# Positional convolution of layer 0: shifted copies taken from DRAM, one load for four channel blocks

## The chip, the cores and the metric

The kernel runs on one core of a Trainium2 chip. Time is the device time of one execution in microseconds (us). The kernel before takes 4210.45 us, the median of three runs (4210.17 to 4224.06).

## The reference, cut to what matters

The network has four layers and works on eight images of 256 channels and 32 x 32 pixels. Layer 0 is an attention block with a convolutional feed-forward part behind it. What the change touches is the line `pe`: a depthwise 3x3 convolution of the values `v`, seen as an image, that is added to the attention's output before the projection.

```python
def _attention(x, ...):
    qkv = _bn(_conv1x1(x, qkv_w), ...).reshape(B, NH, 2 * KD + HD, N)
    q, k, v = (qkv[:, :, :KD], qkv[:, :, KD:2 * KD], qkv[:, :, 2 * KD:])
    attn = softmax(einsum('bhkn,bhkm->bhnm', q, k) * SCALE)
    out = einsum('bhdm,bhnm->bhdn', v, attn).reshape(B, Cc, H, W)
    v_img = v.reshape(B, Cc, H, W)
    pe = _bn(_dwconv3(v_img, pe_w), ...)      # 3x3, one filter per channel
    out = out + pe
    return _bn(_conv1x1(out, proj_w), ...)
```

With B = 8 images, NH = 4 heads, KD = 32 and 64 value channels per head, an image has 256 value channels and N = 1024 pixels. Every output channel of `pe` depends on nine pixels of one input channel.

## The kernel before, in words

Layer 0 is the function `fast0`. Channels lie on the 128 partitions, two tiles of them (c = 0, 1), pixels in the free dimension, and everything is float32. A TensorE instruction of float32 leaves two records in the profile, so the counts of records in it are twice those in the code.

**The loops.** `attention` goes through 128 steps: 8 images, two halves gq of the 512 query columns, eight blocks kt of 128 keys. A step has four score matrix products `s` (L1393; 32 rows x 128 columns of the array each, one per head), two exponentials `e` on ScalarE (L1399), eight products `A` (L1357; 128 rows x 32 columns each, four column groups for the heads, two channel tiles) for the step before, and two sums on VectorE (L1353). `finish` divides by the sums, adds the result to `o`, projects, and stores to `mids`.

`before_attention(b)` prepares an image: it loads it, normalizes it (L1217 squares it into the space of `v`), projects it to `v`, `q`, `k` (L1276 to L1287), transposes `v` (L1297), and then makes the positional convolution into `o`, in four groups (c, h): a channel tile and a half of the pixels. A group works like this. A tile `thrice` of 96 partitions holds three copies of 32 channels, shifted by minus one, zero and plus one image row, for four channel blocks g side by side in the free dimension. GpSimd zeroes the row beyond the image's edge (L1307), SyncE issues twelve loads from `v` in SBUF (L1312; one per shift j and block g, 32 partitions x 512 or 480 pixels), and twelve matrix products `pe` (L1324; 96 rows x 32 columns, three horizontal shifts times four blocks, each block in its own column group) add up all nine taps. ScalarE takes the result out (L1327). There is one buffer for `thrice`, so the copies for a group wait for the products of the group before.

`before_gates`, `gates` and `transforms` are the feed-forward part: a projection `pi`, depthwise filters on VectorE (L1246), a gate, a transfer through DRAM (`gated`), a projection `po` (L1491), and small matrix products for the Fourier filter (`fwd`, `back`).

**The order of the work.** These generators are put side by side by `by_time`: each has a start and a step, and the one that is due next gives the next piece of code. Below that, the framework's scheduler sets the order of instructions on each engine when the program is built, from its own estimate of when each operand is there. Each engine then runs its queue in that fixed order and stops at an instruction whose semaphores are not there. All plain loads and stores of this part go through SyncE's one queue, in order.

In the order as built, the first group of each image and, from image 2 on, the first three groups have their twelve `pe` products together. In the groups 2 to 4 of images 0 and 1 and in the fourth group of the other images, some of them are mixed, one to four at a time, with products `A`, `s` or `po`.

Of the kernel before, what the change touches and what calls it, by code (L numbers as in the profile page):

```python
# [10 lines left out]
F32 = mybir.dt.float32  # L11
# [6 lines left out]
P = 128  # L18
B = 8
C = 256  # L20
KC = C // P
N = 1024
HF = 512
# [113 lines left out]
def img(ap):  # L137
    return ap.rearrange("p (h w) -> p h w", w=IMG)
# [971 lines left out]
def fast0(net, io):  # L1110
    tc, nc = net.tc, net.nc
# [6 lines left out]
    with ExitStack() as ctx, ExitStack() as att:  # L1118
# [6 lines left out]
        awp = io.pool(att, "f0aw", 1)  # L1125
        aone = io.pool(att, "f0aa", 1)
# [7 lines left out]
        g, bb, m, v = (vec[:, i * nb : (i + 1) * nb] for i in range(4))  # L1134
# [13 lines left out]
        s, t = st[:, :nb], st[:, nb:]  # L1148

        wpe = net.load(awp, "f0_wpe").rearrange("p (k t g o) -> p k t g o", k=KC, t=3, g=4)  # L1150
        pib = wp.tile([P, 8], F32, name="pib")
        gain = net.load(wp, "l0_gam2")

        def bank(name):
            return own["X"].tile([P, HF], F32, tag="X", name=name)

        with ExitStack() as tmp:
# [13 lines left out]
            for j in range(8):  # L1171
                for k in range(KC):
                    nc.tensor.matmul(
                        ps[:, 4 + j : 5 + j], lhsT=wpi[:, k, bass.ts(j, P)], rhs=n2b(k),
                        start=(k == 0), stop=(k == KC - 1),
# [25 lines left out]

        qs, ks, vas, os = ({} for _ in range(4))

        mids = [net.dpool.tile([P, KC, N], F32, tag=f"mid{b}", name=f"mid{b}") for b in range(B)]
        gated = [net.dpool.tile([P, 4, 4, 2, P], F32, tag=f"gated{b}", name=f"gated{b}") for b in range(B)]

        def sc(i):
            return s[:, i : i + 1]

        def sh(i):  # L1210
            return t[:, i : i + 1]

        def normed(xn, x, sq):

            squares = [sq(k) for k in range(KC)]
            for k in range(KC):
                nc.scalar.activation(squares[k], x[:, k, :], AF.Square)  # L1217
            yield
            ps = bank("ms")
            for k in range(KC):  # L1220
                for h in range(2):
                    nc.tensor.matmul(
                        ps[64 * h : 64 * h + 64], lhsT=net.mean64, rhs=squares[k][:, bass.ts(h, HF)],
                        start=(k == 0), stop=(k == KC - 1),
                    )
            r = one.tile([P, HF], F32, tag="r", name="r")
            net.rsqrt(r, ps, net.eps6)
            yield
            for h in range(2):
                pr = bank("rb")  # L1230
                nc.tensor.matmul(
                    pr, lhsT=net.unit[64 * h : 64 * h + 1, :], rhs=r[64 * h : 64 * h + 1, :], start=True, stop=True
                )
                nc.scalar.copy(squares[0][:, bass.ts(h, HF)], pr)
            nc.vector.tensor_tensor(xn, x, squares[0].unsqueeze(1).to_broadcast([P, KC, N]), ALU.mult)
# [33 lines left out]
        def before_attention(b):  # L1269
            xn = aone.tile([P, KC, N], F32, tag="xn", name="xn")  # L1270
            nc.sync.dma_start(out=xn, in_=io.src[b])
            yield
            v = aone.tile([P, KC, N], F32, tag="v", name="v")
            yield from normed(xn, xn, lambda k: v[:, k, :])
            yield
            def projected(d, w, j, norm):  # L1276
                for h in range(2):
                    ps = bank("qkv")
                    net.linear(ps, w, xn, bass.ts(j, P), bass.ts(h, HF))
                    nc.scalar.activation(d[:, bass.ts(h, HF)], ps, AF.Identity, scale=sc(norm), bias=sh(norm))  # L1280

            for c in range(KC):
                projected(v[:, c, :], wv, c, 2 + c)
                yield
            for d, (j, name) in ((qs, (0, "q")), (ks, (1, "k"))):
                d[b] = atwo.tile([P, N], F32, tag=name, name=name)
                projected(d[b], wqk, j, j)  # L1287
                yield

            va = vas[b] = atwo.tile([P, NT, KC, P], F32, tag="va", name="va")  # L1290
            for t4 in range(0, NT, 4):
                for t2 in (t4, t4 + 2):
                    ps = bank("vT")
                    for i in range(2):
                        for c in range(KC):
                            lo = i * C + c * P
                            nc.tensor.transpose(ps[:, lo : lo + P], v[:, c, bass.ts(t2 + i, P)], net.ident)  # L1297
                    nc.scalar.copy(va[:, t2 : t2 + 2].rearrange("p t c d -> p (t c d)"), ps)
                yield

            o = os[b] = atwo.tile([P, KC, N], F32, tag="o", name="o")
            for c in range(KC):
                for h in range(2):

                    thrice = aone.tile([96, 4, HF], F32, tag="thrice", name="thrice")
                    edge = thrice[0:32, :, :IMG] if h == 0 else thrice[64:96, :, HF - IMG :]
                    nc.gpsimd.memset(edge, 0.0)  # L1307
                    for j in range(3):
                        n = HF * h + IMG * (j - 1)
                        lo, hi = max(0, n), min(N, n + HF)  # L1310
                        for g in range(4):
                            nc.sync.dma_start(  # L1312
                                out=thrice[32 * j : 32 * j + 32, g, lo - n : hi - n],
                                in_=v[32 * g : 32 * g + 32, c, lo:hi],
                            )
                    yield
                    ps = bank("pe")
                    for j, s_ in enumerate((0, -1, 1)):
                        for g in range(4):
                            to, fr = (  # L1320
                                img(a)[:, :, max(0, -d_) : IMG - max(0, d_)]
                                for a, d_ in ((ps[32 * g : 32 * g + 32], s_), (thrice[:, g, :], -s_))
                            )
                            nc.tensor.matmul(  # L1324
                                to, lhsT=wpe[:96, c, s_ + 1, g, :], rhs=fr, start=(j == 0), stop=(j == 2)
                            )
                    nc.scalar.activation(  # L1327
                        o[:, c, bass.ts(h, HF)], ps, AF.Identity, scale=sc(4 + c), bias=sh(4 + c)
                    )
                    yield  # L1330
                yield
# [189 lines left out]
        for b in range(B):  # L1521
            streams += [
                (T * (b - 1) - 2, 32 / 21, before_attention(b)) if b > 1 else (11 * b, 1.0, before_attention(b)),
                (T * (b + 1) + 7.4, 0.9, before_gates(b)),
                (T * (b + 1) + 10.5, 32 / 44, gates(b)),
                (T * (b + 2) + 11.5, 2, transforms(b)),
            ]
# [1438 lines left out]

GENERAL = [layer0, layer1, layer2_attention, layer2_ffn, layer3_attention, layer3_experts]
LAYERS = [fast0, fast1, fast2, fast2f, fast3, fast3e]
LEAST, MOST = 1e-25, 1e25

# [114 lines left out]
def pack(i):  # L3085

    d = {"x": i["x"].reshape(B, C, N)}
# [40 lines left out]
    p = np.arange(P)  # L3128
# [49 lines left out]
    cols += [_cols(z[n]) for n in ("norm1_w", "norm1_b", "norm2_w", "norm2_b", "gamma1")]  # L3178

    taps = z["pe_w"][v_of].reshape(KC, 4, 32, 3, 3)  # L3180
    wpe = np.zeros((3, 32, KC, 3, 4, 32), np.float32)
    for ch in range(32):
        wpe[:, ch, :, :, :, ch] = taps[:, :, ch].transpose(2, 0, 3, 1)
    d["f0_wpe"] = wpe.reshape(96, -1)
    cols.append(z["dw_w"].reshape(8, P, 9).transpose(1, 0, 2).reshape(P, -1))
    d["f0_vec"] = np.concatenate(cols, 1)

# [48 lines left out]
```

## Time and profile before

| | |
|---|---|
| median of 3 runs | 4210.45 us |
| the profiled execution | 4221.38 us, span 4219.6 us |
| granted TensorE clock, mean | 0.952 |
| layer 0's attention in the span | from about 50 us to beyond 1100 us |
| `pe` products | 768 records, 130.7 us busy |
| period of an image in the middle of the layer | 158 to 160 us |

In the lines of the profile, PE is TensorE's matrix products and PEld its weight loads, DVE VectorE, ACT ScalarE, POOL GpSimd, SPq the queue of SyncE. A line of the timeline gives start and duration in us, the engine, the line of code, the operation with its output and inputs, the shape, and after x how many of them were merged in the line; in brackets stands how long the engine was idle before, and for whom it waited. For a matrix product `96*32` gives the rows and columns of the array that it takes.

### The profile page before, as it was taken

Reading aid. Unit: us, or ns where it says so; the run is one execution under the profiler, and the core shown is the slowest. Engines: PE = TensorE matmul, PEld = TensorE weight load, DVE = VectorE, ACT = ScalarE, POOL = GpSimd, SP = SyncE. Lnnn points to the kernel's source line nnn. Section 1 sums busy time; section 2 is a strip of 40 time slices with the busy share of each in tenths; the row PEclk is TensorE's granted clock in tenths of the full one; section 3 lists DMA queues with packets and bytes.
Section 4 is the critical chain, followed back from the end, with each engine's and each line's share of the span. In section 5 each row is a group of like instructions: output and inputs, shape, how many; then the busy total and the mean of one; then the engine's idle time right before and its main releaser. Section 6 shows DMA issues by size and latency. Waiting matters only on the chain. (4 is left out here: it accounts for less than half of the span.)

```text
span 4219.6 us, 52288 instructions
## 1 busy us (share of the span) xinstructions
PE 3866.5 (92%) x19430; PEld 1900.2 (45%) x19430; DVE 2297.3 (54%) x3994; ACT 2259.1 (54%) x3030; POOL 563.7 (13%) x645
## 2 busy tenths in 40 slices
PE   7999999999987788879999978989899999999997
PEld 3223333333333344444444435654344443436986
DVE  2368878878897488963222255842223333314455
ACT  3455655655554367743433445624655566666554
POOL 0000000000000000000000012440000050124763
PEclk9999999999998788889999989999999999999998
DMA  2222232232212468740100012430700040126676
GB/s 88 62 73 70 73 107 80 73 107 70 70 70 101 147 217 290 254 155 0 41 20 21 22 58 83 148 129 15 226 31 10 27 144 34 36 93 196 197 246 217
DMA packets 212346, 432.70 MB, mean 103 GB/s; under 512 B 26633, under 2 KB 137180, under 8 KB 199668
## 3 DMA queue, kind: packets, MB, share of 16 engines
q1 hardware_dynamic: 188980, 377.70, 27.1%
q0 software_dynamic: 19440, 46.45, 3.3%
q10 hardware_dynamic: 3664, 5.11, 0.4%
q8 instruction: 157, 2.57, 0.3%
q14 instruction: 105, 0.86, 0.1%
HBM read 257.56 MB, written 153.89 MB: 98 GB/s over the span
## 5 line engine op out<-in xcount | busy, mean ns | idle before, releaser
L2690 ACT ACTIVATE e<-s,five 128x1024 f32<-128x1024 f32 x512 | 538.8, 1110 | 277.9 <-PE s L2684 277.0
L1246 DVE SCALAR_TENSOR_TENSOR a<-hp,w_f_vec,a 128x961 f32<-128x961 f32 (+1 forms) x496 | 608.2, 1232 | 104.9 <-ACT a L1239 96.3
L2684 PE MATMUL s<-q,k 32*128 32x512 f32 x2048 | 348.6, 641 | 14.5 <-ACT e L2690 12.0
L1353 DVE TENSOR_TENSOR sum<-sum,e 128x1024 f32<-128x1024 f32 x192 | 230.4, 1218 | 149.2 <-ACT e L1399 149.2
L1399 ACT ACTIVATE e<-s 128x1024 f32<-128x1024 f32 x256 | 249.7, 1022 | 91.5 <-PE s L1393 82.1
L2668 PE MATMUL A<-e,v 128*32 128x512 f32 x2048 | 277.6, 606 | 0.3 <-ACT e L2690 0.3
L1357 PE MATMUL A<-e,va 128*32 128x512 f32 x2048 | 275.8, 620 | 0.0
L78 PE MATMUL pi<-xn,w_l_wpi 128*128 128x512 f32 x512 | 240.1, 610 | 13.7 <-ACT u L1500 9.2
L2684 PEld LDWEIGHTS s<-q,k 32*128 32x128 f32 x2048 | 111.4, 183 | 177.4 <-issue 94.2
L1393 PE MATMUL s<-q,k 32*128 32x512 f32 x1024 | 182.2, 648 | 2.4 <-ACT e L1399 2.4
L2837 PE MATMUL h<-xk,w 128*128 128x128 f32 x1192 | 152.7, 283 | 13.8 <-DVE xk L2823 13.8
L1704 PE MATMUL acc<-wt,z 128*64 128x192 f32 (+4 forms) x1344 | 128.5, 335 | 39.8 <-DVE wt L1759 39.3
L1026 POOL DMA_INDIRECT res<-y,to x149 | 148.6, 997 | 110.5 <-DVE y L2861 58.2
L78 PEld LDWEIGHTS pi<-xn,w_l_wpi 128*128 128x128 f32 x512 | 93.6, 193 | 149.5 <-issue 112.1
L2837 PEld LDWEIGHTS h<-xk,w 128*128 128x128 f32 x1192 | 150.6, 199 | 18.9 <-DVE xk L2823 14.1
L2806 ACT COPY w<-w_l3f_w 128x512 f32 x149 | 92.6, 625 | 115.8 <-PE h L2837 111.3
L1307 POOL MEMSET thrice<- 32x128 f32 x32 | 6.3, 196 | 1072.6 <-PE pe L1324 1072.6
L1438 ACT ACTIVATE hp<-pi,pib 128x512 f32<-128x512 f32 x128 | 87.1, 690 | 115.9 <-PE pi L78 115.9
L1324 PE MATMUL pe<-thrice,w_f_wpe 96*32 96x496 f32 (+1 forms) x768 | 130.7, 615 | 17.0 <-DMA thrice<-v 10.2
L2857 PE MATMUL y<-w_l3f_w,hid 128*128 x596 | 142.2, 381 | 0.3 <-ACT hid L2843 0.3
L1026 POOL DMA_INDIRECT so<-xl,rows x128 | 129.8, 1014 | 91.2 <-issue 50.4
L1357 PEld LDWEIGHTS A<-e,va 128*32 128x32 f32 x2048 | 61.9, 112 | 175.9 <-issue 175.3
(406 smaller groups left out, 6978.6 us busy)
## 6 DMA issues: line engine op xcount, KB each, us to landing
row<-shifts SPq DMA_DIRECT2D x144, 512.0 KB
x<-d SPq DMA_DIRECT2D x31, 1024.0 KB
xs<-so SPq DMA_DIRECT2D x73, 260.0 KB
so<-zero SPq DMA_DIRECT2D x5, 3380.0 KB
thrice<-v SPq DMA_DIRECT2D x256, 64.0 KB
gated<-st SPq DMA_DIRECT2D x32, 512.0 KB
hc<-gated SPq DMA_DIRECT2D x32, 512.0 KB
xl<-mox SPq DMA_DIRECT2D x64, 256.0 KB
```

Source lines behind the costliest of these rows:

```text
L78: self.nc.tensor.matmul(ps, lhsT=w[:, i, m], rhs=src[:, i, cols], start=(i == 0), stop=(i == k - 1))
L1026: made = self.nc.gpsimd.indirect_dma_start(**args)
L1246: nc.vector.scalar_tensor_tensor(to, fr, taps(t_), to, ALU.mult, ALU.add)
L1353: nc.vector.tensor_tensor(half, half, e[j], ALU.add)
L1357: nc.tensor.matmul(state["A"][32 * h : 32 * h + 32, c, :], lhsT=vas[b][:, kt, c, 32 * h : 32 * h + 32], rhs=e[h // 2][:, h % 2, :], start= ...
L1393: nc.tensor.matmul(ss[h // 2][:, h % 2], lhsT=ks[b][32 * h : 32 * h + 32, bass.ts(kt, P)], rhs=qs[b][32 * h : 32 * h + 32, bass.ts(gq, HF) ...
L1399: nc.scalar.activation(es[i][j], ss[j], AF.Exp, scale=SCALE)
L2668: nc.tensor.matmul(A[32 * h : 32 * h + 32], lhsT=v[:, kt, c * P + 32 * h : c * P + 32 * h + 32], rhs=e[:, h, :], start=first, stop=last,)
L2684: nc.tensor.matmul(ss[h // 2][:, h % 2], lhsT=k[32 * h : 32 * h + 32, c, bass.ts(kt, P)], rhs=q[32 * h : 32 * h + 32, c, bass.ts(hh, HF)], ...
L2690: nc.scalar.activation(e[:, 2 * j : 2 * j + 2], ss[j], AF.Square, scale=SCALE, bias=five)
L2837: nc.tensor.matmul(ps[:, j, m], lhsT=ws[j][:, k, bass.ts(m, P)], rhs=xk[:, j, k], start=(k == 0), stop=(k == KC - 1),)
L2857: nc.tensor.matmul(ps[:, j, :], lhsT=hid[:, j, k, :], rhs=w[:, k, :], start=(k == 0), stop=(k == KC - 1))
```

## The change

- The values go to DRAM: behind the projection of each channel tile, `v[:, c, :]` (128 x 1024, 512 KB) is stored to a new DRAM tile `stored[b][c]`.
- A group's twelve loads become three, one per shift j. Each reads 32 channels x 4 blocks x 512 or 480 pixels from DRAM, and writes all four blocks of one shift.
- `thrice` is one tile for the whole layer, with 128 rows instead of 96, zeroed once; rows 96 to 127 stay zero. The weights get 32 zero rows, and the twelve `pe` products take 128 rows of the array.

The zeroing of the edge, the number of `pe` products, and the single buffer stay.

```diff
+        thrice = awp.tile([P, 4, HF], F32, name="thrice")
+        nc.gpsimd.memset(thrice.rearrange("p g n -> p (g n)"), 0.0)
...
+        stored = [net.dpool.tile([KC, P, N], F32, tag=f"vimg{b}", name=f"vimg{b}") for b in range(B)]
...
                 projected(v[:, c, :], wv, c, 2 + c)
+                nc.sync.dma_start(out=stored[b][c], in_=v[:, c, :])
...
-                    thrice = aone.tile([96, 4, HF], F32, tag="thrice", name="thrice")
                     edge = thrice[0:32, :, :IMG] if h == 0 else thrice[64:96, :, HF - IMG :]
                     nc.gpsimd.memset(edge, 0.0)
                     for j in range(3):
                         n = HF * h + IMG * (j - 1)
                         lo, hi = max(0, n), min(N, n + HF)
-                        for g in range(4):
-                            nc.sync.dma_start(
-                                out=thrice[32 * j : 32 * j + 32, g, lo - n : hi - n],
-                                in_=v[32 * g : 32 * g + 32, c, lo:hi],
-                            )
+                        nc.sync.dma_start(
+                            out=thrice[32 * j : 32 * j + 32, :, lo - n : hi - n],
+                            in_=stored[b][c].rearrange("(g p) n -> p g n", g=4)[:, :, lo:hi],
+                        )
...
-                                to, lhsT=wpe[:96, c, s_ + 1, g, :], rhs=fr, start=(j == 0), stop=(j == 2)
+                                to, lhsT=wpe[:, c, s_ + 1, g, :], rhs=fr, start=(j == 0), stop=(j == 2)
...
-    wpe = np.zeros((3, 32, KC, 3, 4, 32), np.float32)
+    wpe = np.zeros((4, 32, KC, 3, 4, 32), np.float32)
     for ch in range(32):
-        wpe[:, ch, :, :, :, ch] = taps[:, :, ch].transpose(2, 0, 3, 1)
-    d["f0_wpe"] = wpe.reshape(96, -1)
+        wpe[:3, ch, :, :, :, ch] = taps[:, :, ch].transpose(2, 0, 3, 1)
+    d["f0_wpe"] = wpe.reshape(P, -1)
```

## The prediction

> **What bounds the kernel now.** I read the page first, then the groups of the lines that the diff touches, then the windows of one image, and last the timeline around the groups of `pe` products, because shares alone don't tell what they cost.
>
> ```profile
> PE 3866.5 (92%) x19430; PEld 1900.2 (45%) x19430; DVE 2297.3 (54%) x3994; ACT 2259.1 (54%) x3030; POOL 563.7 (13%) x645
> ...
> L1324 PE MATMUL pe<-thrice,w_f_wpe 96*32 96x496 f32 (+1 forms) x768 | 130.7, 615 | 17.0 <-DMA thrice<-v 10.2
> ```
>
> TensorE is busy nearly always, and the products in question take 130.7 us and waited only 10.2 us for their copies. On this reading there is little to win. The window of one image (us, then busy time of PE, PEld, DVE, ACT, POOL, then clock, DMA share and GB/s) says who bounds this stage:
>
> ```profile
> 725.20:883.17 157.97, 149.29 (x753) 57.94 (x753) 130.18 (x121) 93.21 (x118) 0.78 (x4) 0.99 0.27 87
> ```
>
> TensorE 149.3 of 158.0 us, VectorE 130.2, ScalarE 93.2: what TensorE's queue loses is lost for the layer, and VectorE has 28 us per image in reserve. Now the timeline, first a group whose twelve products (24 records) stand together:
>
> ```profile
> 54.30 2.73 PE L1324 MATMUL pe<-thrice,w_f_wpe 96*32 96x512 f32 x24
> 56.96 1.14 PE L1393 MATMUL s<-q,k 32*128 32x512 f32 x8
> 58.03 1.92 PE L1357 MATMUL A<-e,va 128*32 128x512 f32 x16
> 59.88 1.37 PE L1393 MATMUL s<-q,k 32*128 32x512 f32 x8
> ```
>
> From start to start: a whole group 2.66 us, `s` 1.07, `A` 1.85, so a step of attention 2.92. Next, from image 1, a group that is mixed with `s`:
>
> ```profile
> 147.13 1.12 PE L1393 MATMUL s<-q,k 32*128 32x512 f32 x2
> 148.19 1.05 PE L1324 MATMUL pe<-thrice,w_f_wpe 96*32 96x512 f32 x2
> 149.16 1.12 PE L1393 MATMUL s<-q,k 32*128 32x512 f32 x2
> ```
>
> One `s` product alone takes 1.06 us, as long as four together, and one `pe` product 0.97 us: each crossing between the two shapes pays a full pass. And from the fourth group of image 5, with SyncE's queue:
>
> ```profile
> 762.78 5.58 SPq L1312 DMA_DIRECT2D thrice<-v  x9
> ...
> 768.83 0.60 SPq L1388 DMA_DIRECT2D mid<-x  x1
> ...
> 770.28 1.92 PE L1357 MATMUL A<-e,va 128*32 128x512 f32 x16
> ...
> 770.73 0.59 SPq L1514 DMA_DIRECT2D d<-xc  x1
> ...
> 771.37 1.88 SPq L1312 DMA_DIRECT2D thrice<-v  x3
> ...
> 772.02 1.02 PE L1324 MATMUL pe<-thrice,w_f_wpe 96*32 96x512 f32 x2
> ...
> 773.59 1.02 PE L1324 MATMUL pe<-thrice,w_f_wpe 96*32 96x512 f32 x2 [0.55 <-DMA thrice<-v]
> ...
> 774.54 0.70 PE L1491 MATMUL po<-w_l_wpo,hc 128*128 128x256 f32 x2
> ...
> 775.17 1.05 PE L1324 MATMUL pe<-thrice,w_f_wpe 96*32 96x512 f32 x2
> ...
> 776.15 1.13 PE L1491 MATMUL po<-w_l_wpo,hc 128*128 128x256 f32 x4
> ...
> 777.21 2.71 PE L1324 MATMUL pe<-thrice,w_f_wpe 96*32 96x512 f32 x18
> ...
> 779.85 2.43 PE L1491 MATMUL po<-w_l_wpo,hc 128*128 128x256 f32 x10
> ...
> 782.20 1.14 PE L1393 MATMUL s<-q,k 32*128 32x512 f32 x8
> ```
>
> `A`, the group and eight `po` products take 11.92 us, most of which TensorE counts as busy. The page hides this: a stretched product is busy time. Three of twelve loads stood in the queue behind a store that waited for VectorE.
>
> [...]LDWEIGHTS: [...]the trace has 112 ns for 96x32 (L1324) and 112 ns for 128x32 (L1357). [...]the load `xn` (L1421) waits 2.5 us at most for the store `mid` before it, 15.0 us over six times.
>
> **The change part by part.**
>
> *Fewer issues.* Twelve issues of 0.63 us (5.58 us for nine) are 7.5 us per group; three are 1.9. The bytes stay at 752 KB. For the wide load I have no row of this very shape; loads with 2 KB rows moved some 340 KB per us in this stage by the transfers' records, and first bytes came 1.3 us after the issue. So a group's copies are there 0.1 + 1.9 + 1.3 + 0.8 + 0.3 = 4.4 us after the products that free the buffer (estimate from those), instead of 9.5. Bounds: 4 us, if the last load finds the path empty, and 7 us, if scattered rows halve the rate.
>
> *The order on TensorE.* This is the large term. As the changed program is built, all 32 groups have their twelve products together; five times a group falls inside a step's `s` products, which adds a crossing of 1.06 us, except in image 0's first group, where half a step stood apart before too. VectorE's order is the same throughout, TensorE's and ScalarE's are the same behind the last group, so layers 1 to 3 are untouched. I rebuild each mixed stretch from the prices above.
>
> - Image 0, 53.24 to 96.52: 43.3 us. Six steps 17.5, four groups 10.6, half a step's `s` 1.06, a split 1.06: 30.3. Less 13.0.
> - Image 1, 131.60 to 184.46: 52.9 us. Six steps 17.5, four groups 10.6, `proj` 3.6 (135.34 to 138.97), a split 1.06: 32.9. Less 20.0, of which 4.0 are waits for copies, and 1.7 a group at half clock.
> - Image 2, fourth group, 289.76 to 307.78: 18.0 us at a granted clock of 0.72. `A` 1.85, `s` 1.07, group 2.66, split 1.06: 6.6. Less 11.4, minus 1.06 for a new split in its second group: 10.3.
> - Images 3 to 7, fourth group: 11.92 us. `A` 1.74 (770.28 to 772.02), group 2.66, eight `po` 3.65 (1117.90 to 1121.55): 8.05. Less 3.9 each, 19.4.
>
> Sum 62.7 us. It needs copies in time. In image 0, between the end of one group and the start of the next lie two steps, some 6 us, against 4.4. In image 1 the third load of group 2 stands behind the store `mid`, which waits for VectorE until 141.0; it lands by about 144.1, and the group is due at 145. Both just fit; if the true figure is 7 us, images 0 and 1 give back some 1.5 us at each of six groups, 9 us.
>
> Not all of it will arrive. Where TensorE doesn't stall, the chain `s`, `e`, `s` of 2.9 us through ScalarE (1.94 us for two `e`) is as long as the step, and the filters on VectorE come in unbroken runs (17.5 us from 325.09). What is late next is VectorE, which stood idle 8.0 us before 784.43 for a late `e`, and 12.6 us in three gaps between 298 and 313: these gaps take most of the shift. I keep four fifths of the 43.3 of images 0 to 2, and nine tenths of the 19.4: 52 us.
>
> *The round trip through DRAM.* Two more stores per image (512 KB), and the first load of an image stands on SyncE until the store has landed, some 2.5 us. Queued behind it: the second store, a `gated` store, two loads, then `mid`. In image 5 `v` is ready at 670.3 and 676.5, so these are out by 679, and `mid` waits for VectorE until 685.2 anyway. The group itself comes some 55 us later. In image 0 the loads land near 48 and the group starts after 54. Cost nothing; without this cover 2.5 us per image, 20 us.
>
> *`v` is free earlier.* ScalarE's squares waited 18.3 us in seven times for the last copy out of `v`. That goes, but off TensorE's path: 0 to 5 us; I count 0.
>
> *128 rows, zeroing, larger weights.* One product's shortest time is 577 ns at 96 rows and 496 columns, and 590 at 128 rows and 512 columns (`A`), a difference that the columns explain: nothing. The one-time zeroing ends long before 43 us. 96 KB more weights stand before the image on SyncE: 0.3 us.
>
> The profiled execution took 4221.4 us, so 4169 for its like. It was 11 us over the median; against 4210.45 I predict **4158 us**.
>
> **The rivals.** (1) *Only the stalls of images 0 to 2 turn into time*, and from image 3 on VectorE is the real bound: its 130.2 of 158.0 us leaves gaps that it may need. Then 25 to 35 us, 4180. Against: its 8 us gap at the very place. (2) *Nothing measurable*: ScalarE's chain or later work takes up what TensorE leaves, or the layer's end hangs on VectorE, which is busy 94% in the window from 1188 to 1300: 0 to 20 us, 4200. Against: its inputs come from TensorE. (3) *Slower*: SyncE's queue becomes the wait. The loads behind the store have 685.2 - 679 = 6.2 us in reserve before they hold `mid` and with it `xn` and the next norm (ScalarE already waited 10.1 us for `xn` from `mid`, six times). If a store lands not after 2.5 but after more than 8.7 us, each further us costs all eight images 1 us: at 15 us the gain is gone, at 18 us the kernel takes 4230. Against: six landings of that kind of store at 2.5 us at most. (4) The change not doing what it says: twelve loads do become three in the order as built; this is excluded.
>
> **How the numbers follow.** Forecast (40 us or more gained) 0.66, rival 1 0.19, rival 2 0.10, rival 3 0.05. The likeliest case by itself spans 4140 to 4172: all 62.7 us and some of ScalarE's waits at one end, three fifths at the other. The range for 8 in 10 reaches over rival 1: 4135 to 4194. Half a per cent, 21 us, is what a measurement here can tell from no change: faster 0.85, within 0.10, slower 0.05.
>
> **What would show it.** In the changed profile: 32 groups of 24 records in 2.5 to 3.0 us; busy time of `pe` near 90 instead of 130.7; 96 issues of 0.6 us instead of 384; the wait of `pe` for copies under 10 us; the period of an image near 154 instead of 158 to 160; the fourth group with `A` and `po` near 8. The prediction is wrong if groups wait longer for wide loads, if the period stays at 158, or if the fourth group gets short and a wait for VectorE appears behind it.

## The result, and the profile after

The changed kernel takes 4164.23 us (median of six runs, 4153.68 to 4178.96), the kernel before on the same chip 4224.61 us (4210.17 to 4233.77). The ratio is 0.9866, with a 95% interval of 0.9835 to 0.9896: 1.3% faster, some 56 us by the ratio and 60 by the two medians. The forecast was 4158 us, 52 us less.

The engines on the profile page of the changed kernel (its profiled execution took 4178.96 us, span 4177.1):

```profile
PE 3826.0 (92%) x19430; PEld 1887.8 (45%) x19430; DVE 2298.4 (55%) x3994; ACT 2260.1 (54%) x3030; POOL 566.3 (14%) x646
```

TensorE's busy time fell by 40.5 us with the same number of instructions. The largest part is in one group of instructions (its busy time and mean ns, then the idle time before it):

```profile
L1326 PE MATMUL pe<-thrice,w_f_wpe 128*32 128x496 f32 (+1 forms) x768 | 88.7, 587 | 3.4 <-issue 3.4
```

It was 130.7 us with 17.0 us of idle time, 10.2 of it for the copies; now the profile puts no wait of a `pe` product on a copy. One group probably still had such a wait: the second of image 1 starts after 1.03 us of idle time that the profile puts on nothing, and its third load had gone out 4.4 us before, behind the store `mid`. (The products `A` that stood between them fell from 275.8 to 263.0 us; the other lines rose by some 14 us together.) The timeline of TensorE in image 0 shows it: two steps of attention between two whole groups.

```profile
56.74 2.73 PE L1326 MATMUL pe<-thrice,w_f_wpe 128*32 128x512 f32 x24
59.40 1.13 PE L1395 MATMUL s<-q,k 32*128 32x512 f32 x4
60.46 1.92 PE L1359 MATMUL A<-e,va 128*32 128x512 f32 x16
62.31 1.14 PE L1395 MATMUL s<-q,k 32*128 32x512 f32 x8
63.38 1.92 PE L1359 MATMUL A<-e,va 128*32 128x512 f32 x16
65.24 1.36 PE L1395 MATMUL s<-q,k 32*128 32x512 f32 x6
66.53 2.73 PE L1326 MATMUL pe<-thrice,w_f_wpe 128*32 128x512 f32 x24
```

From the end of one group to the start of the next are 7.06 us, and TensorE doesn't stand before the second: the copies were there. And the fourth group of image 5 (it runs in the window of image 4), on TensorE:

```profile
724.99 1.92 PE L1359 MATMUL A<-e,va 128*32 128x512 f32 x16
726.73 2.71 PE L1326 MATMUL pe<-thrice,w_f_wpe 128*32 128x512 f32 x24
729.36 3.72 PE L1493 MATMUL po<-w_l_wpo,hc 128*128 128x256 f32 x16
733.01 1.14 PE L1395 MATMUL s<-q,k 32*128 32x512 f32 x8
```

and on SyncE's queue before it:

```profile
717.50 1.25 SPq L1314 DMA_DIRECT2D thrice<-vimg  x3
...
723.88 0.57 SPq L1390 DMA_DIRECT2D mid<-x  x1
```

`A`, group and `po` take 8.02 us from 724.99 to 733.01, where they took 11.92. All three loads go out in 1.25 us, ahead of the store `mid` that waits for VectorE, where three of twelve stood behind it.

What this is worth for an image shows in its window (time, busy time of PE, PEld, DVE, ACT, POOL, then granted clock, DMA share and GB/s). In the first trace of the changed kernel:

```profile
754.85:911.79 156.94, 147.27 (x753) 57.38 (x753) 130.06 (x122) 93.26 (x118) 0.78 (x4) 0.98 0.29 94
```

That is 1.0 to 2.6 us less than an image before (157.97 and 159.5), not 3.9. Two of the forecast's sums thus stood in doubt after the first trace: images 0 to 2 had given 47 us instead of 35, images 3 to 7 some 3 us instead of 17.5. Two more executions of the same kernel, below, answer that.

### The profile page after: what moved, and what is told of

Its sections match the earlier page's. It is cut to its first block, busy times and chain, and to the rows that moved or that the text cites. A ratio compares the mean times of both kernels' runs of the same rounds, so it can differ in the third digit from the quotient of the medians.

```text
span 4177.1 us, 51736 instructions
## 1 busy us (share of the span) xinstructions
PE 3826.0 (92%) x19430; PEld 1887.8 (45%) x19430; DVE 2298.4 (55%) x3994; ACT 2260.1 (54%) x3030; POOL 566.3 (14%) x646
## 5 line engine op out<-in xcount | busy, mean ns | idle before, releaser
L78 PE MATMUL pi<-xn,w_l_wpi 128*128 128x512 f32 x512 | 249.0, 629 | 19.2 <-ACT v L1283 10.0
L1359 PE MATMUL A<-e,va 128*32 128x512 f32 x2048 | 263.0, 610 | 0.0
L1706 PEld LDWEIGHTS acc<-wt,z 128*64 128x64 f32 x1344 | 97.7, 151 | 89.5 <-DVE wt L1761 60.1
```

The costliest lines, as they stand in the source:

```text
L78: self.nc.tensor.matmul(ps, lhsT=w[:, i, m], rhs=src[:, i, cols], start=(i == 0), stop=(i == k - 1))
L1359: nc.tensor.matmul(state["A"][32 * h : 32 * h + 32, c, :], lhsT=vas[b][:, kt, c, 32 * h : 32 * h + 32], rhs=e[h // 2][:, h % 2, :], start= ...
L1706: nc.tensor.matmul(acc[o, a * IMG : e * IMG], lhsT=zs[b][:, c, t, :], rhs=wt[:, c, (a - lo) * IMG : (e - lo) * IMG], start=False, stop=(t ...
```

## The experiments

The theory was the prediction's: TensorE's time goes where `pe` products are mixed with `s` and `po`, and fewer, faster loads let the groups stand together without waiting. The rivals: it is only the order, or only the source and the queue; the 128 rows matter; the round trip costs; VectorE is the bound from image 3 on.

### The changed kernel again

No edit; the measure for the three kernels that follow.

> The changed kernel itself once more, as the measure for the other kernels beside it. Both theories: 0.987 of the kernel before, as measured (0.9835 to 0.9896); about 48 us less at the end of layer 0's attention, of which images 0 to 2 give about 45 and images 3 to 7 about 3 together.

Measured 4169.6 us against 4227.99, ratio 0.9861 (0.9835 to 0.9886). Its trace differs from the first in the middle images, which take 155.0, 153.9, 155.4 and 154.8 us instead of 156.8 to 156.9. The split of the gain that I had expected from the first trace is missed: images 0 to 2 gave about 42 us, images 3 to 7 about 16.

### The order alone: the last load is needed first

```
-                        for g in range(4):
+                        for g in reversed(range(4)):
```

> The kernel before, in which only the order of the four loads of a shift is turned round, so that the group's first product needs the last of the twelve loads. As built, the twelve products of each of the 32 groups then stand together on TensorE; the copies still come from SBUF, in twelve loads of 0.63 us each. Theory (the unmixed order is what gains, and the faster loads are what make it affordable): groups of 24 records in 2.7 us, but in images 0 and 1 the group now waits for copies that land 9.5 us after the buffer is free where two steps are only 6 us, so some six waits of 3 to 5 us; 15 to 30 us less than before, ratio 0.993 to 0.9965. Rival a (the order alone gives all of it, the DRAM copy nothing): 0.987, as the changed kernel. Rival b (the shorter SyncE queue and the source give it, the order nothing): 1.000 or more.

Measured 4211.33 us, ratio 0.9956 (0.994 to 0.9972), inside the theory's bounds and outside both rivals'. The group of instructions, and three groups of the timeline:

```profile
L1324 PE MATMUL pe<-thrice,w_f_wpe 96*32 96x496 f32 (+1 forms) x768 | 104.8, 651 | 24.9 <-DMA thrice<-v 12.1 <-issue 11.8 <-ACT a L1239 0.9
```

```profile
66.33 3.06 PE L1324 MATMUL pe<-thrice,w_f_wpe 96*32 96x512 f32 x24 [1.96 <-DMA thrice<-v]
...
78.47 5.58 PE L1324 MATMUL pe<-thrice,w_f_wpe 96*32 96x512 f32 x24 [1.97 <-issue]
...
146.17 4.66 PE L1324 MATMUL pe<-thrice,w_f_wpe 96*32 96x512 f32 x24 [1.57 <-DMA thrice<-v]
```

The products stand together and `pe` is busy for 104.8 us instead of 130.7, but TensorE stands 1.6 to 2.0 us before each of these groups. For the first and third the profile names the loads as the reason; before the second it names nothing. The second then runs at half clock throughout and the third in part (granted clock 0.50 and 0.63). The order alone gives 0.44%, a third of the gain. This trace itself shows less: up to the last `s` of layer 0 it gains 3 us on the kernel before, and its images 3 to 6 take 160.2 to 160.4 us. (The order isn't quite the changed kernel's: eleven times instead of five a group stands inside a step's `s`, which costs a crossing: two of the four `s` products alone take 1.06 us, 59.40 to 60.46 in the timeline of image 0 above, and all four 1.07, 62.31 to 63.38.)

### The source alone: twelve loads from DRAM

```
+                nc.sync.dma_start(out=stored[b][c], in_=v[:, c, :])
...
-                                in_=v[32 * g : 32 * g + 32, c, lo:hi],
+                                in_=stored[b][c][32 * g : 32 * g + 32, lo:hi],
```

> The kernel before with v stored to DRAM and the shifted copies loaded from there, but still in twelve loads of a group, 96 rows. As built the products of a group stand mixed with s and po again. Theory (order and number of loads decide, the source nothing): 0.997 to 1.003 of before, pe busy near 130 us again. Rival (what counts is that v comes free early and that the copies are read from DRAM): 0.987 to 0.990. Rival 3 of the prediction (the landing of the store holds SyncE): slower than before, 1.003 to 1.006.

Measured 4219.68 us, ratio 0.9982 (0.9968 to 0.9997): at most 0.3% of the 1.4%. The fourth group of an image is mixed as before, on the timeline from 769.0:

```profile
770.77 1.02 PE L1326 MATMUL pe<-thrice,w_f_wpe 96*32 96x512 f32 x2
773.39 1.02 PE L1326 MATMUL pe<-thrice,w_f_wpe 96*32 96x512 f32 x2 [1.59 <-issue]
774.34 0.70 PE L1493 MATMUL po<-w_l_wpo,hc 128*128 128x256 f32 x2
774.96 1.60 PE L1326 MATMUL pe<-thrice,w_f_wpe 96*32 96x512 f32 x2
776.49 2.08 PE L1493 MATMUL po<-w_l_wpo,hc 128*128 128x256 f32 x4
778.50 2.81 PE L1326 MATMUL pe<-thrice,w_f_wpe 96*32 96x512 f32 x18
781.24 2.43 PE L1493 MATMUL po<-w_l_wpo,hc 128*128 128x256 f32 x10
```

and the window of the image in which it stands:

```profile
644.76:805.42 160.66, 150.93 (x753) 58.57 (x752) 130.21 (x122) 93.08 (x118) 0.78 (x4) 0.98 0.29 92
```

TensorE is busy for 150.93 us with the same products as the changed kernel's 147.27, both with two half-clock stretches: 3.7 us for the mixed group, close to the 3.9 that the prediction had rebuilt. Earlier release of `v` and the DRAM source by themselves are worth nearly nothing. Neither the order alone nor the source alone makes the gain; order, source and three loads in place of twelve together do. What the number of loads is worth by itself is not shown, because the turned order with twelve loads from DRAM was not run. An issue takes 0.45 us on the mean in this trace and 0.60 in the one with loads from SBUF, so twelve would be out some 1.8 us sooner (an estimate from these), nearly as much as TensorE stood before the groups shown with the turned order.

### 96 rows instead of 128

```
-        thrice = awp.tile([P, 4, HF], F32, name="thrice")
-        nc.gpsimd.memset(thrice.rearrange("p g n -> p (g n)"), 0.0)
+        thrice = awp.tile([96, 4, HF], F32, name="thrice")
...
-                                to, lhsT=wpe[:, c, s_ + 1, g, :], ...
+                                to, lhsT=wpe[:96, c, s_ + 1, g, :], ...
...
-    wpe = np.zeros((4, 32, KC, 3, 4, 32), np.float32)
+    wpe = np.zeros((3, 32, KC, 3, 4, 32), np.float32)
...
```

> The changed kernel with the copy and the weights on 96 rows, as before; the rest, and the order on every engine, as changed. Theory (128 rows cost and bring nothing): 0.997 to 1.003 of the changed kernel, so 0.985 to 0.990 of before, one pe product at its shortest 577 ns in both. Rival [...]: groups longer than 3 us, and half of the gain or more gone, 0.993 or more of before.

Measured 4170.26 us beside the changed kernel's 4169.6 on the same chip; ratio to before 0.9847 (0.9822 to 0.9872). The shortest product takes 577 ns in both. The rows make no difference that these runs could show.

### The trip through DRAM twice

```
+        first = [net.dpool.tile([KC, P, N], F32, tag=f"vfst{b}", name=f"vfst{b}") for b in range(B)]
...
-                nc.sync.dma_start(out=stored[b][c], in_=v[:, c, :])
+                nc.sync.dma_start(out=first[b][c], in_=v[:, c, :])
+                nc.sync.dma_start(out=stored[b][c], in_=first[b][c])
```

> The changed kernel with v going to DRAM twice: v to a first buffer, from there to the one that the copies are loaded from, so SyncE waits for two landings per half of an image instead of one. Theory (the landing is covered by the 6.2 us that the queue has ahead of mid, and by the 55 us to the group): some 2.5 us more on SyncE per trip, 0 to 5 us slower than the changed kernel, 0.986 to 0.989 of before. Rival 3 of the prediction (SyncE's queue sits on the path): 2.5 us or more per image, at least 20 us slower than the changed kernel, 0.991 or more of before.

Measured 4226.51 us on a chip where the kernel before takes 4280.23: ratio 0.986 (0.9824 to 0.9896), the changed kernel's. What SyncE's queue waited for in this kernel (us in total, times, longest):

```profile
SPq L1289 <- DMA vfst<-v: 36.7, 16, 4.4
...
SPq L1316 <- DMA vimg<-vfst: 8.3, 4, 3.7
```

The queue stands for 45 us for landings, against 21.7 us in the changed kernel (eight times, 2.7 us on the mean, 4.7 at the longest). The ratio is the changed kernel's, so the 20 us of the rival are excluded: the cover that the prediction named was real. A few us are not excluded. In its one trace the doubled trip is 4 to 12 us behind the changed kernel's traces up to the last `s`.

### VectorE relieved, in both kernels

Both leave out one tap of the depthwise filters (eight of nine are summed), once on the changed kernel and once on the kernel before:

```
-            for t_ in (0, 1, 2, 3, 5, 6, 7, 8):
+            for t_ in (0, 1, 2, 3, 5, 7, 8):
```

> The changed kernel with one of the eight taps that VectorE works out in the depthwise filters of layer 0 left out (the filters sum eight taps instead of nine), so some 9.8 us less on VectorE in each image. To be read against the next kernel, which leaves out the same of the kernel before. Theory (from image 3 on VectorE takes back what TensorE gained): with VectorE relieved an image gains 3.5 us or more by the change instead of 2, and the two kernels lie 55 to 66 us apart. Rival (half-clock stretches of TensorE take it back, VectorE has nothing to do with it): still 1.5 to 2.5 us per image, 44 to 52 us apart.

> The kernel before with the same tap left out on VectorE. Theory (TensorE bounds the kernel before with its mixed groups): an image falls by at most 3 us from 158.5, 10 to 25 us in all, ratio 0.994 to 0.998 of before. Rival (VectorE bounds already before): it falls by 5 to 9 us per image, 40 to 70 us, ratio 0.983 to 0.990.

Measured 4195.42 us (ratio 0.9789, 0.9755 to 0.9824) for the changed kernel without the tap, and 4260.22 us (0.9954, 0.9935 to 0.9972) for the one before. They lie 64.8 us apart, as the theory expected, but the two intervals leave some 17 us to either side, so against the 56 to 60 us of the whole kernels this settles nothing. The windows do better. First without the tap after the change, then without it before:

```profile
440.02:593.35 153.33, 145.53 (x753) 56.65 (x752) 121.11 (x113) 93.21 (x118) 0.79 (x4) 0.99 0.30 96
```

```profile
644.02:801.55 157.53, 149.20 (x753) 58.25 (x752) 121.15 (x113) 93.20 (x118) 0.78 (x4) 0.99 0.27 87
```

Against images with the same clock in whole kernels (153.87 us after, 157.97 before), 9 us less on VectorE bring 0.4 to 0.5 us. VectorE is not the bound of an image, before or after, and the second kernel's rival falls with that. Its gain over the kernel before is 4.7 us up to the last `s`; from there to the layer's last `back`, where VectorE is busy 94% of a window, it gains another 8.5. My theory that VectorE takes back the gain falls too: the change gives an image 4.2 us with VectorE relieved (157.53 and 153.33) and 4.1 us without (157.97 and 153.87).

### The sum of image and attention on GpSimd

```
-                nc.vector.tensor_tensor(x, x, av, ALU.add)
+                nc.gpsimd.tensor_tensor(x, x, av, ALU.add)
```

> The changed kernel with the sum of image and attention (x + av, ahead of the store mid) on GpSimd instead of VectorE, the same computation. As built, the fourth group of an image is then split by po products again. Theory (VectorE bounds a part of each image): 0 to 2 us less per image from VectorE, but 3 to 4 us lost at the fourth group: 0 to 15 us slower than the changed kernel, 0.986 to 0.990 of before. Rival (VectorE's relief is worth more than the order): faster than the changed kernel, below 0.984.

Measured 4246.68 us, ratio 0.9917 (0.9883 to 0.995): 20 us slower than the doubled trip on the same chip, which ran like the changed kernel, and more than I expected. The fourth group is a part, though not by being split by `po`: on the chip its products stand together, as in image 5:

```profile
745.61 1.13 PE L1395 MATMUL s<-q,k 32*128 32x512 f32 x4
748.37 2.73 PE L1326 MATMUL pe<-thrice,w_f_wpe 128*32 128x512 f32 x24 [1.63 <-DMA thrice<-vimg]
751.03 3.72 PE L1493 MATMUL po<-w_l_wpo,hc 128*128 128x256 f32 x16
```

But its third load stands behind the store `mid` again, TensorE waits 1.5 to 1.9 us for it in each of images 3 to 7, and the group cuts a step's `s` in two. Another part I hadn't thought of; VectorE's filters as one line's instructions (ns least, median, longest), in the changed kernel and in this one:

```profile
L1249 DVE SCALAR_TENSOR_TENSOR a<-hp,w_f_vec,a x496: 1189/1226/1255, 213.3 to 1338.7; 128x961 f32<-128x961 f32 x85, 128x992 f32<-128x992 f32 x81
```

```profile
L1249 DVE SCALAR_TENSOR_TENSOR a<-hp,w_f_vec,a x496: 1207/1246/3326, 216.6 to 1373.9; 128x961 f32<-128x961 f32 x83, 128x992 f32<-128x992 f32 x83
```

The same 496 instructions take 635.5 us instead of 609.1, so VectorE lost 26.4 us and shed only 16 sums of 1.22 us. The loss lies where GpSimd adds: the 25 filter instructions that overlap one of its sums take 2.27 us on the mean, the other 471 take 1.23 as in the changed kernel.

### The changed kernel a third time, and before a second time

> The changed kernel once more, beside the two that follow, and as a third execution's trace. Two traces of it so far show images of 156.9 us (with two stretches of half clock in each) and of 153.9 to 155.4 us (with one or two). Theory (images 3 to 7 gained 4.1 us each at full clock, and what a single trace loses of that are half-clock stretches): again between 153.3 and 157 us, and 1.7 us between images that differ by one such stretch; 0.985 to 0.989 of before. Rival (VectorE bounds an image at 156.9): 156 us or more in nearly all images.

> The kernel before once more, for a second trace of it to stand against the three of the changed kernel. Theory (an image's period is 158.0 us with one half-clock stretch and 159.5 with two, 4.1 us above the changed kernel's 153.9 and 155.4): images 3 to 6 between 157.5 and 160 us, the last s some 58 us later, counted from the first, than the 1139.6 us of the changed kernel's second and third trace. Rival (the first trace of before was a slow one, and the change gives less): images below 157 us and the last s less than 52 us later.

Measured 4170.19 us for the changed kernel beside 4225.12 (0.9873, 0.9836 to 0.9909). The kernel before took 4280.19 us, on another chip; up to the last `s` its two traces agree, with images of 158.0, 159.5, 159.6 and 161.0 us in the second, one of them above what was expected. From the first `s` of layer 0 (start of image 0) in us:

| trace | to image 3 | image 3 to the last `s` | sum |
|---|---|---|---|
| before, first and second | 436.8, 433.9 | 760.7, 763.5 | 1197.5, 1197.4 |
| after, second and third | 395.1, 395.0 | 744.7, 744.5 | 1139.7, 1139.5 |
| after, first; with 96 rows | 389.7, 389.7 | 757.6, 757.5 | 1147.3, 1147.2 |

So these four traces of the changed kernel (one with 96 rows) show two patterns, each repeated to 0.2 us, 7.7 us apart; one gains 57.9 us, the other 50.2. The same order of instructions stands behind both. In images 0 to 2 the first trace's pattern is 5 us ahead; in images 3 to 7 it is 13 us behind, and in the middle images there one wait, that of `pi`, differs. First the first trace, then the third (timeline of TensorE in image 5):

```profile
782.62 1.14 PE L1395 MATMUL s<-q,k 32*128 32x512 f32 x8
786.00 5.40 PE L78 MATMUL pi<-xn,w_l_wpi 128*128 128x512 f32 x8 [2.24 <-ACT v L1283]
```

```profile
782.71 1.14 PE L1395 MATMUL s<-q,k 32*128 32x512 f32 x8
784.81 3.70 PE L78 MATMUL pi<-xn,w_l_wpi 128*128 128x512 f32 x8 [0.96 <-ACT v L1283]
```

Where `pi` stalls for 2.24 us instead of 0.96, the eight products then take 5.40 us instead of 3.70: 1.28 us of wait and 1.70 us of half clock. The windows of the third trace, two images and those `pi` products:

```profile
599.54:753.41 153.87, 145.60 (x753) 56.57 (x752) 130.13 (x122) 93.14 (x118) 0.78 (x4) 0.99 0.30 96
753.41:908.93 155.52, 147.23 (x753) 57.16 (x752) 130.12 (x121) 93.15 (x118) 0.78 (x4) 0.98 0.30 95
784.81:788.35 3.54, 3.54 (x8) 1.63 (x9) 2.64 (x4) 3.03 (x4) 0.00 (x0) 1.00 0.79 263
```

The first image has one half-clock stretch, the second two, and TensorE's busy time differs by 1.63 us. Before the change an image takes 157.97 us with one and 159.5 with two. Like with like, the change gives some 4.1 us per image, also in the other pattern: before's image of 161.0 us has the long wait of `pi`, as the first trace's of 156.9 have. The expectation's rival (156 us in nearly all images) falls: with VectorE fully loaded images of 153.9 us occur, twice in the same places.

What goes with the patterns can be read from the clock. In each of the fourteen traces the half-clock stretches of layer 0 start on one grid of 3.413 us (to 0.003 us) and last whole steps of it, 3.41, 6.83, 10.24 us and so on. `D`, another product, waits 2.33 us in each image. In image 5 of the first trace this wait, from 766.12 to 768.46, is cut by a boundary of the grid at 766.73; in the third trace, from 764.69 to 767.03, it lies within one step. The steps around it, first trace, then third:

```profile
763.32:766.73 3.41, 2.81 (x15) 0.87 (x13) 2.82 (x4) 2.46 (x3) 0.00 (x0) 1.00 0.00 0
766.73:770.14 3.41, 1.68 (x16) 0.55 (x20) 3.30 (x4) 2.71 (x5) 0.00 (x0) 1.00 0.00 0
```

```profile
764.34:767.75 3.41, 1.07 (x10) 0.29 (x12) 2.97 (x3) 3.12 (x5) 0.00 (x0) 1.00 0.00 0
767.75:771.16 3.41, 3.41 (x20) 0.65 (x12) 3.38 (x3) 1.23 (x2) 0.00 (x0) 0.50 0.01 2
```

Twelve of the traces have this wait of `D` in each of images 3 to 6, so 48 times. It lies within one step 18 times, and half clock follows each time; of the 30 that a boundary cuts, 11 are followed by it. In the 29 images with half clock behind `D`, `pi` waits 0.96 us; in the 19 without, 2.24 us. In image 5, counted from its start, TensorE comes to `pi` after 28.91 us in the first trace and 30.44 in the third, and ScalarE releases it after 31.15 and 31.40. So the pattern goes with the place of `D` on the grid, in kernels with and without the tap alike. No run moved the grid on purpose.

### Two attempts at TensorE's remaining stalls

In both patterns `D` waits 2.3 us for one of two PSUM banks (PSUM is where this kernel's products are put), which the two halves of `rb`, a product of the norm, hold until ScalarE has copied them (the profile ends the wait of 2.33 us with that copy, L1237). One kernel puts a step of other work between the halves, the other puts `D` a step later:

```
                 nc.scalar.copy(squares[0][:, bass.ts(h, HF)], pr)
+                yield
```

```
                 nc.scalar.copy(av, A)
                 yield
+                yield
                 D = bank("D")
...
                 yield
-                yield
                 for c in range(KC):
```

> The changed kernel with one step of other work between the two halves of the broadcast rb in each norm, so that these do not hold both of the two PSUM banks at once while ScalarE is busy with e; as built, all 32 groups are whole and none is split from s. Theory (the stall of 2.3 us of D for the bank, the 1.2 us of vT, and the half-clock stretches that follow such stalls, are what keeps an image above 153 us): 2 to 5 us less per image than the changed kernel, ratio 0.976 to 0.983 of before. Rival (the stall just moves to another product, or VectorE takes it): 0.984 to 0.989.

> The changed kernel with the product D, which waits 2.3 us for a bank that rb holds, one step of attention later (and the step between D and proj shorter by one). As built, a group is split once, and proj, vT and pi take other places. Theory (the stall of D and the half-clock stretch behind it cost the image): 1 to 4 us less per image than the changed kernel, 0.979 to 0.985 of before. Rival (the wait moves to proj, which now comes sooner behind D): 0.985 to 0.992.

Measured 4193.82 us (0.9924, 0.9898 to 0.995) and 4208.83 us (0.9961, 0.995 to 0.9972): both slower than the changed kernel, by more than their rivals said. In the middle images `D` no longer waits for 2.3 us in either. With `D` a step later the wait turned up not at `proj`, as the rival had it, but at `qkv`, which waits 2.8 us for `xn`, and `pi` waits 2.1 us. With the extra step between the halves a longer wait turned up elsewhere, on TensorE's timeline:

```profile
653.77 1.92 PE L1360 MATMUL A<-e,va 128*32 128x512 f32 x16
660.62 1.98 PE L1225 MATMUL ms<-sq,mean 128*64 128x512 f32 x4 [4.93 <-ACT sq L1220]
```

and the windows behind it have the clock at half for over 13 us:

```profile
660.62:664.53 3.91, 3.91 (x7) 0.80 (x7) 0.00 (x0) 0.89 (x1) 0.00 (x0) 0.50 0.63 199
664.53:669.95 5.42, 5.42 (x14) 1.30 (x13) 0.35 (x1) 2.73 (x4) 0.00 (x0) 0.50 0.85 246
669.95:674.00 4.05, 4.05 (x6) 1.84 (x6) 2.01 (x2) 1.24 (x3) 0.00 (x0) 0.50 0.49 126
```

Neither beats the changed kernel.

## Why the prediction was right, and where a step was off

**What bounds.** Right. TensorE's lost time was the bound: of the 50.2 us that the first trace gains up to the last `s`, 41.8 are busy time of TensorE (1114.6 and 1072.8 us) and 8.4 its idle time, while VectorE and ScalarE are as busy as before (899 and 672 us).

**Fewer issues.** Right in direction, the price too high: three loads go out in 1.25 us, not 1.9 (one issue took 0.39 us in the median, where I had carried over the 0.6 of loads from SBUF). The 4.4 us for the copies can't be read directly. They were there without a wait in the shortest gap between two groups, 5.89 us. The one group of image 1 that was said to fit just so probably did not, by 1.0 to 1.2 us.

**The order on TensorE.** Right in the sum: the built order held on the chip. In the first trace 30 of the 32 groups take 2.7 us; two share the array with `A` and take 3.44 and 3.55. That mixture is cheap, one `A` product among `pe` products adding 0.7 to 0.9 us, so the price of a crossing belongs to `pe` against `s` or `po`, which the prediction did price. In the trace before, from start to start at full clock, a single `s` product ahead of `pe` takes 1.05 us (six times), a single `pe` ahead of `po` 0.97 to 0.98 (five times), and a single `pe` ahead of `A` 0.09 to 0.28 (three times). The fourth group takes 8.02 us with `A` and `po` (predicted 8.05). Not all that stands under this heading is order, though. Of image 0's 13.0 us, 5.3 were waits for copies and some 3.4 half clock (an estimate: half of the two stretches of 3.41 us at 64.3 and 77.95), and of image 2's 10.3 a wait was 2.6 and half clock some 5; the copies that came in time took these away. That fits the small gain of the order alone.

**What is kept.** The sum was 62.7 us, the forecast kept 34.6 of images 0 to 2 and 17.5 of images 3 to 7. Against the mean of the two traces before, the second and third trace give 40.3 and 17.5, the first 45.6 and 4.5. So 57.8 of the rebuilt 62.7 us arrived in two traces and 50.1 in the other, and the cause named for the loss was wrong. It is not VectorE's gaps: an image moves by 0.5 us when VectorE is relieved. What the traces show instead are waits of TensorE of 2 us and more and the half clock that follows many of them. In the third trace, for instance, `qkv` of image 1 waits 2.50 us for `xn` and its sixteen records then take 10.19 us, where eight `pi` records of the same shape take 3.70. I had used the half clock in the stretches before the change (0.72 in image 2), and counted none behind it. In the first trace this, with the longer wait of `pi`, leaves only 4.5 us of what images 3 to 7 could gain; the forecast's period "near 154" holds for two traces of three. That the whole-kernel forecast came so near is in part luck: four fifths was too little for images 0 to 2 in every trace, and where `D` falls on the clock's grid was not foreseen.

**The round trip, 128 rows, `v`.** Right, each by its own run: doubling the trip and going back to 96 rows don't move the ratio clear of its interval (0.25 to 0.4% to either side), which leaves room for several us, and the source alone moves it by 0.2%. A weight load of 32 rows and 128 columns (`s`) takes 185 ns on the mean in the trace before, one of 32 columns 112 with 96 rows (`pe`) as with 128 (`A`). A landing took 2.7 us on the mean and 4.7 at the longest (2.5 forecast).

**The rivals.** The first (only images 0 to 2 gain, VectorE bounds) names the place of the gain in the first trace (45.6 of 50.1 us in images 0 to 2), though not its size, 25 to 35 us, and is wrong in its reason: relieving VectorE by 9 us moves an image by 0.5 us, and the executions with 4.1 us gained have VectorE just as busy. Nothing measurable, and SyncE's queue as the wait, are excluded by the result and by the doubled trip.

## What to carry to other kernels

Price a mixed stretch of matrix products by the starts on the timeline, not by busy or idle time: here a product alone between two of another shape took some 1 us, as long as four together, and all of it looked like work. To keep such products together, all their operands must be there at once and early, which here was a matter of how long a group's transfers take to issue (1.25 us for three, 5.58 for nine of twelve) and of what they stand behind in the queue (the store `mid`); the order without the faster transfers gave a third of the gain. And compare images of equal granted clock, or several traces, before naming a cause for two or three microseconds per image.

## What the runs showed of the hardware

- In the twelve traces with `D`'s wait of 2.33 us, the wait lay within one step of the clock's grid of 3.413 us 18 times and was followed by half clock 18 times; where a boundary of the grid cut it, 11 times of 30. One such stretch lasts 3.41 us, and two images or two sets of `pi` products that differ by one differ by 1.63 and 1.70 us of TensorE's busy time. A wait of 4.93 us was followed by over 13 us of half clock. The grid lies differently under the same instructions in two executions (a boundary of it 11.88 us after the start of image 5 in the first trace, 10.93 and 14.34 in the third), and keeps its place through layer 0 in each (to 0.003 us). What sets its place, and which other waits would do, is not shown.
- GpSimd's sum of 128x1024 takes 2.72 us (median of 16), VectorE's 1.22, and VectorE's filters beside GpSimd's sums are up to 3.33 us long where the longest is 1.26 in the changed kernel. The filters took 26.4 us more over the layer, all of it in the 25 instructions beside those sums; what makes them longer is not shown.
